# Layer 1's attention product of a four-layer graph network: one product with 128 stationary columns, or two with 64

## The chip, the core and the metric

The kernel runs on one core of a Trainium2 chip. The metric is the device time of one execution, in microseconds (us). The kernel before takes 2623.5 us, the median of three runs (2618.03 to 2626.04). A core has a matrix engine (TensorE, PE in the profile, with its weight loads as PEld), three engines for elementwise work (VectorE or DVE, ScalarE or ACT, GpSimd or POOL), queues that start DMA transfers, an on-chip memory with 128 partitions, and a smaller one, PSUM, into which TensorE writes. A product on TensorE has a stationary operand, loaded first, and a moving operand, streamed through it. The number of columns of the stationary is the number of partitions of the result; the columns of the moving operand are the result's columns.

## What is computed

Sixteen graphs of 1024 nodes go through four layers, x of 1024 x 256 values a graph, with a 0/1 adjacency matrix of 1024 x 1024. Each layer takes `h = relu(layernorm(x))` and adds its result to x. The change is in layer 1:

```python
Wh = jnp.einsum('bnd,de->bne', h, W)
f_i = Wh @ a1
f_j = Wh @ a2
e = jax.nn.leaky_relu(f_i[:, :, None] + f_j[:, None, :], negative_slope=0.2)
e = jnp.where(adj > 0, e, NEG_INF)
alpha = jax.nn.softmax(e, axis=-1)
out = jnp.einsum('bij,bjd->bid', alpha, Wh)
x = x + jax.nn.elu(out)
```

Layer 0 is the same with the softmax over the other axis. Layer 2 averages a linear map of the neighbours and adds a second map. Layer 3 is attention with four heads of 64 columns and a layer norm of its own.

## The kernel before

Everything is in float32. Nodes are cut into NT = 8 blocks of 128, one node of each block to a partition. A graph's layer 1 (`layer1`, line 798) has three phases. First, eight projections (`project`, L686) give `hs`, the rows of Wh with two more columns for f_i and f_j; ScalarE scales them out of PSUM (L802). Then f_j of all nodes is turned into one row, sent through DRAM and broadcast to all partitions (L699 to L711). Then come the weights and the products. For each block j of neighbours VectorE makes `p`, 128 x 1024, one instruction (L822): the exponentials of the masked logits, with neighbours j in the partitions and all 1024 nodes i along the row. ScalarE scales block j of `hs` by a factor of its node (L820); column D of `hs` holds that factor itself, so that the product's last column is the softmax's sum.

The product of output block i sums over j: stationary the 128 columns of `p` that belong to block i, moving the 257 columns of `hs[:, j]`, accumulated in one PSUM bank over the eight j (`product`, line 814, L815). The first two output blocks (EARLY = 2) are multiplied as soon as each `p` is there, so that these products stand among the making of the p's; the other six follow, eight products each. PSUM has two banks for these results (`at_ps`). Each result is read by VectorE (reciprocal of the sum, L836) and by ScalarE twice (L838, L840), and goes to `residual` (line 727). That adds it to x on VectorE (L736, L737), and after every second block starts the next layer's norm: sums of squares on ScalarE (L640), shift and ReLU into `hn` (L667), and TensorE transposes of `hn` (`flip`, L680), whose result ScalarE copies out (L681).

Layer 3's product (line 942) already has the form that the change gives to layer 1. For each p (L929) and each block i, a loop `for c in range(2)` multiplies the 64 columns of `part` of the stationary, with 65 moving columns, into partitions 0 to 63 or 64 to 127 of the result. Layer 0's product (line 759), the projections (L686) and layer 2's products (L877, L883) have stationaries of 128 columns.

All sixteen graphs are generators. Each yields an estimate of the time of the piece just written; a queue ordered by due time (line 1051) resumes the one that is due, and graphs start 120 units apart (`APART`). So layer 1 of one graph is written among layer 3 of the graph before, and its later part beside that graph's tail (line 954) and the first pieces of the graph after it. The framework's planner then orders each engine's instructions by that program order and by what it takes to be ready, and places the waits; instructions wrapped in `later` stay in program order. On each engine the resulting order is fixed. `layer1` yields 1.35 after each block of p and 3.74 after each output block. The mask steps (L575), ScalarE's conversion of the adjacency matrix as it arrives by DMA on the SP queue, belong to the next graph and stand among this on ScalarE's queue.

Of the kernel before, what the change touches and what calls it, by code (L numbers as in the profile page):

```python
# [14 lines left out]
P = 128  # L15
# [406 lines left out]
def tile_simple_stack(  # L422
# [11 lines left out]
    nc = tc.nc  # L434
    B, N, D = x.shape
    NT = N // P
# [246 lines left out]
    def project(norm, w, n, width):  # L683
        ps = mm_ps.tile([P, HALF], F32, tag="mm", name="ps_proj")
        for c in range(DC):
            nc.tensor.matmul(ps[:, :width], norm.ht[:, c, n * P : (n + 1) * P], w[:, c, :width], start=(c == 0), stop=(c == DC - 1))  # L686
        return ps

    def new_hs(name="hs"):
        return state.tile([P, NT, W3], F32, tag="hs", name=name, bufs=3)  # L690

    def spread(col, n, scales, name):

        k = n * NT
        ps = tr_ps.tile([P, P], F32, tag="tr", name="ps_col")
        nc.tensor.transpose(ps[:k, :], col, ident)  # L699
        all_rows = []  # L700
        for scale in scales:
            e = small.tile([H * NT, P], F32, tag="e_row", name="e_row", bufs=2)
            nc.scalar.activation(e[:k, :], ps[:k, :], AF.Exp, scale=scale)
            d = dram.tile([n, N], F32, tag=f"row_{name}", name="d_row", bufs=4)
            later(nc.sync.dma_start(d.rearrange("r (t p) -> (r t) p", p=P), e[:k, :]))
            all_rows += [d[r] for r in range(n)]
        return all_rows

    def everywhere(d, tag):
        row = work.tile([P, N], F32, tag=tag, name="row", bufs=2)  # L710
        later(nc.sync.dma_start(row, d.partition_broadcast(P)))  # L711
        return row

    def column(src, n):

        col = small.tile([P, H, NT], F32, tag="col", name="col", bufs=2)
        nc.vector.tensor_copy(col[:, :n, :], src.rearrange("p t n -> p n t"))
        return col[:, :n, :].rearrange("p n t -> p (n t)")

    def watch(b, layer, terms):  # L720
        k = b * 3 + layer
        nc.vector.tensor_reduce(top[:, k : k + 1], terms, axis=AX.XY, op=OP.max, apply_absolute_value=True)

    def weights(name):
        return work.tile([P, N], F32, tag="p", name=name, bufs=NT)

    def residual(xs, i, v, after, e=None):

        x = xs[:, i, :]
        if i % 2 == 0:  # L730
            if i == NT - 2:
                after.settle()
            after.flip()
            after.sums = small.tile([P, 2], F32, tag="sums", name="sums")
        if e is not None:
            nc.vector.scalar_tensor_tensor(x, e, 1.0, x, op0=OP.min, op1=OP.add)  # L736
        nc.vector.scalar_tensor_tensor(x, v, 0.0, x, op0=OP.max, op1=OP.add, accum_out=after.sums[:, i % 2 : i % 2 + 1])  # L737
        if i % 2:
            after.pair(xs, i // 2, after.sums)
# [58 lines left out]
    def layer1(b, xs, mask, norm, after):  # L798
        hs = new_hs()
        for n in range(NT):  # L800
            ps = project(norm, wx[1], n, D + 2)
            nc.scalar.activation(hs[:, n, : D + 2], ps[:, : D + 2], AF.Copy, scale=norm.rs[n])  # L802
            yield 1.05
        (d_row,) = spread(column(hs[:, :, D + 1 : D + 2], 1), 1, (S - 1.0,), "l1")
        row = everywhere(d_row, "row")
        watch(b, 1, hs[:, :, D : D + 2])
        q = small.tile([P, NT], F32, tag="q", name="q")
        nc.scalar.activation(q, hs[:, :, D], AF.Exp, scale=1.0 - S)
        nc.scalar.activation(hs[:, :, D], hs[:, :, D], AF.Exp, scale=S)
        yield 8.0  # L810
        ps_ = []
        early = [at_ps.tile([P, HALF], F32, tag="at", name="ps_o1") for _ in range(EARLY)]

        def product(ps, i, j):
            nc.tensor.matmul(  # L815
                ps[:, : D + 1], ps_[j][:, i * P : (i + 1) * P], hs[:, j, : D + 1], start=(j == 0), stop=(j == NT - 1)
            )

        for j in range(NT):
            nc.scalar.activation(hs[:, j, :D], hs[:, j, :D], AF.Copy, scale=hs[:, j, D : D + 1])  # L820
            p = weights("p1")
            nc.vector.scalar_tensor_tensor(p, row, q[:, j : j + 1], mask[:, j, :], op0=OP.max, op1=OP.mult)  # L822
            ps_.append(p)
            for i, ps in enumerate(early):
                product(ps, i, j)
            yield 1.35
        for i in range(NT):
            if i < EARLY:
                ps = early[i]
            else:  # L830
                ps = at_ps.tile([P, HALF], F32, tag="at", name="ps_o1")
                for j in range(NT):
                    product(ps, i, j)
            k = b * NT + i
            z = shares[:, k : k + 1]
            nc.vector.reciprocal(z, ps[:, D : D + 1])  # L836
            e = work.tile([P, D], F32, tag="e", name="e")
            nc.scalar.activation(e, ps[:, :D], AF.Exp, scale=z)  # L838
            v = work.tile([P, D], F32, tag="v", name="v")
            nc.scalar.activation(v, ps[:, :D], AF.Copy, scale=z)  # L840
            residual(xs, i, v, after, e)
            yield 3.74
# [232 lines left out]
    ps = tr_ps.tile([P, P], F32, tag="tr", name="ps_bad")  # L1075
# [64 lines left out]
```

## Time and profile before

| | us |
|---|---|
| median of three runs | 2623.5 |
| lowest, highest | 2618.03, 2626.04 |
| span of the profiled execution | 2619.6 |
| TensorE matmul busy (share) | 2456.4 (94%) |
| TensorE weight load busy | 2094.9 (80%) |
| VectorE busy | 1965.3 (75%) |
| ScalarE busy | 1439.9 (55%) |
| layer 3's products, L942, busy | 541.6 |
| layer 1's products, L815, busy | 494.3 |
| layer 0's products, L759, busy | 494.0 |

The span runs from the first to the last instruction of one profiled execution; its time lies between the lowest and the highest of the runs. A float32 product is two instructions in the trace. A row of a group gives the line, the engine, the operation, the operands, the stationary's partitions x columns, the moving operand's partitions x columns, the count, then busy us, the mean ns of one, and the engine's idle time before it with what ended it. The length of one matmul includes its way through the array, and the next starts before it ends, so the time that one costs in a row of them is the distance of two starts. A line of a timeline gives start and length in us of a run of like instructions.

### The profile page before, as it was taken

The numbers are of one execution on the slowest core, as the hardware profiler recorded it, in microseconds if no ns is written. First come the engines' busy times: TensorE is split into PE (matmuls) and PEld (weight loads), VectorE is DVE, ScalarE is ACT, GpSimd is POOL, SyncE is SP. The second block draws the span as 40 slices with busy tenths as digits, with TensorE's granted clock in tenths as the row PEclk, the third lists the DMA queues.
The fourth block names the chain that finished last, engine by engine and source line by source line (L and its number), as shares of the span: only waits on it lengthen the run. The fifth ranks groups of instructions, "written<-read, shape, count | busy, mean of one in ns | idle before, by whom it ended". The sixth has DMA issues, their size and how long they took to land.

```text
span 2619.6 us, 63024 instructions
## 1 busy us (share of the span) xinstructions
PE 2456.4 (94%) x26194; PEld 2094.9 (80%) x26194; DVE 1965.3 (75%) x3815; ACT 1439.9 (55%) x4065; POOL 449.5 (17%) x454
## 2 busy tenths in 40 slices
PE   5799999999999999999999999999999999999975
PEld 4688888888878888787888878888888888878864
DVE  4457778687687977778687787877778687787858
ACT  4564755637565473755637565473755637565350
POOL 1010211203112030211203112030211203011021
PEclk8899999999999999999999999999999999999997
DMA  4541442616225251331615225251432615224021
GB/s 144 126 85 54 107 85 62 133 59 144 53 76 126 70 133 55 108 83 62 134 58 144 57 76 122 70 133 54 124 67 64 137 59 140 66 71 101 26 65 36
DMA packets 212632, 233.76 MB, mean 89 GB/s; under 512 B 10416, under 2 KB 161072, under 8 KB 212336
## 3 DMA queue, kind: packets, MB, share of 16 engines
q1 hardware_dynamic: 74608, 145.73, 17.5%
q0 software_dynamic: 137728, 83.90, 17.5%
q8 instruction: 208, 3.41, 0.5%
q14 instruction: 88, 0.72, 0.1%
HBM read 212.35 MB, written 17.24 MB: 88 GB/s over the span
## 4 chain that ended last, share of the span: by engine, by line
PE 56%; DVE 16%; DMA 12%; ACT 11%; issue 3%; POOL 2%; SPq 0%; DVEq 0%; POOLq 0%; ACTq 0%
PE ps_o L759 15%; PE ps_proj L686 12%; PE ps_o L942 9%; DVE p L929 6%; PE ps_o L883 6%; PE ps_o L815 6%; DMA row<-d_row 5%; PE pt_h L680 5%; DMA raw<-in_adj_t 4%; DVE p L822 4%; ACT mask L575 3%; PE ps_o L877 3%; ACT hn L667 2%; DMA d_row<-e_row 2%; ACT unread L640 2%
## 5 line engine op out<-in xcount | busy, mean ns | idle before, releaser
L929 DVE SCALAR_TENSOR_TENSOR p<-row,q,mask 128x1024 f32<-128x1024 f32 x512 | 631.9, 1278 | 65.4 <-PE ps_o L942 55.7
L942 PEld LDWEIGHTS ps_o<-hb,p 128*64 128x64 f32 x16384 | 505.5, 138 | 102.0 <-DVE p L929 41.2
L942 PE MATMUL ps_o<-hb,p 128*64 128x65 f32 x16384 | 541.6, 224 | 28.9 <-DVE p L929 20.8
L759 PE MATMUL ps_o<-hs,p 128*128 128x256 f32 x2048 | 494.0, 386 | 26.4 <-ACT hs L773 26.0
L686 PE MATMUL ps_proj<-wx,ht 128*128 128x258 f32 (+2 forms) x2048 | 507.8, 388 | 4.0 <-ACT hs L746 2.3
L815 PE MATMUL ps_o<-hs,p 128*128 128x257 f32 x2048 | 494.3, 388 | 14.5 <-ACT mask L575 7.7
L759 PEld LDWEIGHTS ps_o<-hs,p 128*128 128x128 f32 x2048 | 379.7, 191 | 82.8 <-ACT hs L773 30.3
L815 PEld LDWEIGHTS ps_o<-hs,p 128*128 128x128 f32 x2048 | 373.9, 190 | 69.9 <-ACT mask L575 8.3
L686 PEld LDWEIGHTS ps_proj<-wx,ht 128*128 128x128 f32 x2048 | 365.8, 190 | 79.6 <-ACT hs L746 10.4
L592 POOL TENSOR_SCALAR rs<-mv 128x4 f32<-128x4 f32 (+1 forms) x112 | 40.6, 362 | 1555.3 <-ACT unread L640 1542.1
L593 POOL TENSOR_TENSOR rs<-rs,neg_half 128x4 f32<-128x4 f32 (+2 forms) x144 | 261.6, 1818 | 11.7
L736 DVE SCALAR_TENSOR_TENSOR xs<-e,xs 128x256 f32<-128x256 f32 x256 | 108.0, 422 | 182.2 <-ACT e L791 134.1
L667 ACT ACTIVATE hn<-xs,shift 128x256 f32<-128x256 f32 x384 | 175.3, 502 | 123.6 <-DVE shift L635 123.6
L680 PE MATMUL pt_h<-ident,hn 128*128 128x128 f32 x1024 | 180.9, 287 | 43.4 <-ACT hn L667 42.4
L575 ACT ACTIVATE mask<-raw 128x512 uint8<-128x512 int32 x256 | 160.1, 627 | 86.7 <-DMA raw<-in_adj_t 59.5
L883 PE MATMUL ps_o<-hi,adj 128*128 128x258 f32 x1024 | 202.9, 321 | 1.6
L680 PEld LDWEIGHTS pt_h<-ident,hn 128*128 128x128 f32 x1024 | 115.1, 142 | 111.1 <-ACT hn L667 95.0
L585 POOL DMA_DIRECT2D adj<-in_adj x128 | 114.6, 896 | 480.3 <-PE ps_o L883 478.6
L737 DVE SCALAR_TENSOR_TENSOR xs<-v,xs 128x256 f32<-128x256 f32 x384 | 161.0, 422 | 29.5 <-ACT v L793 16.2
L769 DVE SCALAR_TENSOR_TENSOR p<-row,q 128x1024 f32<-128x1024 f32 x128 | 161.4, 1270 | 25.1 <-DMA row<-d_row 25.1
L950 ACT ACTIVATE res<-ps_o 128x260 f32<-128x260 f32 x128 | 46.5, 375 | 228.0 <-PE ps_o L942 227.7
L822 DVE SCALAR_TENSOR_TENSOR p<-row,q,mask 128x1024 f32<-128x1024 f32 x128 | 156.9, 1279 | 10.3 <-DMA row<-d_row 10.1
(108 smaller groups left out, 3000.1 us busy)
## 6 DMA issues: line engine op xcount, KB each, us to landing
raw<-in_adj_t SPq DMA_DIRECT2D x256, 256.0 KB
adj<-in_adj POOLq DMA_DIRECT2D x128, 512.0 KB, 4.9
row<-d_row SPq DMA_DIRECT2D x112, 512.0 KB
xs<-in_x POOLq DMA_DIRECT2D x32, 512.0 KB, 7.1
out<-xs SPq DMA_DIRECT2D x32, 512.0 KB
wx<-in_w SPq DMA_DIRECT2D x3, 256.0 KB
d_row<-e_row SPq DMA_DIRECT2D x48, 4.0 KB
wts<-in_w_t SPq DMA_DIRECT2D x2, 256.0 KB
```

What stands on the lines that cost most here:

```text
L575: nc.scalar.activation(self.bytes[:, n, g * HALF : (g + 1) * HALF], raw, AF.Square, accum_out=squares[:, k : k + 1])
L593: nc.gpsimd.tensor_tensor(rs[:, :n], rs[:, :n], neg_half[:, :n], op=OP.pow)
L667: nc.scalar.activation(hn, xs[:, 2 * g + k, :], AF.Relu, scale=scale, bias=bias)
L680: nc.tensor.transpose(pt[:, c, k * P : (k + 1) * P], hn[:, c * P : (c + 1) * P], ident)
L686: nc.tensor.matmul(ps[:, :width], norm.ht[:, c, n * P : (n + 1) * P], w[:, c, :width], start=(c == 0), stop=(c == DC - 1))
L759: m = nc.tensor.matmul(ps[:, :D], ps_[j][:, i * P : (i + 1) * P], hs[:, j, :D], start=(j == 0), stop=(j == NT - 1))
L769: nc.vector.scalar_tensor_tensor(p, row_a, q[:, j : j + 1], row_b, op0=OP.mult, op1=OP.max)
L815: nc.tensor.matmul(ps[:, : D + 1], ps_[j][:, i * P : (i + 1) * P], hs[:, j, : D + 1], start=(j == 0), stop=(j == NT - 1))
L822: nc.vector.scalar_tensor_tensor(p, row, q[:, j : j + 1], mask[:, j, :], op0=OP.max, op1=OP.mult)
L883: nc.tensor.matmul(ps[:, : D + 2], adj_n[j][:, i, :], h[:, i, : D + 2], start=False, stop=(h is lo and i == NT - 1), skip_group_check=True,)
L929: nc.vector.scalar_tensor_tensor(p, row, q[:, jj, h : h + 1], mask[:, jj, :], op0=OP.max, op1=OP.mult)
L942: nc.tensor.matmul(pss[g][part, k * HW : (k + 1) * HW], ps_[t][:, i * P : (i + 1) * P][:, part], hbv[:, j + t, h, :], start=(j == 0 and t ...
```

## The change

`product` in `layer1` becomes a loop over two halves. Half c takes columns 64c to 64c + 63 of the stationary block and writes partitions 64c to 64c + 63 of the same PSUM bank, with the same moving operand. The results and all that reads them are as before; there are 2048 products in place of 1024, which is 4096 matmul instructions in place of 2048.

```diff
         def product(ps, i, j):
-            nc.tensor.matmul(
-                ps[:, : D + 1], ps_[j][:, i * P : (i + 1) * P], hs[:, j, : D + 1], start=(j == 0), stop=(j == NT - 1)
-            )
+            for c in range(2):
+                part = slice(c * P // 2, (c + 1) * P // 2)
+                nc.tensor.matmul(
+                    ps[part, : D + 1], ps_[j][:, i * P : (i + 1) * P][:, part], hs[:, j, : D + 1],
+                    start=(j == 0), stop=(j == NT - 1),
+                )
```

## The prediction

> **What bounds the kernel now.** I read the page's busy times first, then the groups of instructions by shape, a table of stages, and TensorE's timeline. The page:
>
> ```profile
> PE 2456.4 (94%) x26194; PEld 2094.9 (80%) x26194; DVE 1965.3 (75%) x3815; ACT 1439.9 (55%) x4065; POOL 449.5 (17%) x454
> ```
>
> TensorE is busy 94% of the span, so what the change does to TensorE's time counts, unless it falls in a stretch where another engine is the limit. The groups by shape, for layer 1's product (L815) and layer 3's (L942):
>
> ```profile
> L942 PE MATMUL ps_o<-hb,p 128*64 128x65 f32 x16384 | 541.6, 224 | 28.9 <-DVE p L929 20.8 <-ACT res L950 4.3 <-issue 2.7
> L815 PE MATMUL ps_o<-hs,p 128*128 128x257 f32 x2048 | 494.3, 388 | 14.5 <-ACT mask L575 7.7 <-DVE p L822 5.9 <-ACT v L840 0.7
> ```
>
> The code issues 16 x 8 x 8 = 1024 products in layer 1 and the trace has 2048 matmuls, so each float32 product is two instructions. Layer 1's part in a graph (157 us apart) falls into three stages; the table gives for graph 5 the window, its length, and busy us of PE, PEld, DVE, ACT and POOL:
>
> ```profile
> 879.00:903.00 24.00, 22.67 (x425) 18.91 (x421) 23.96 (x39) 4.81 (x15) 0.00 (x0) 1.00 0.13 47
> 903.00:917.00 14.00, 12.77 (x62) 10.93 (x63) 12.86 (x26) 12.35 (x36) 0.87 (x2) 1.00 0.45 142
> 917.00:928.00 11.00, 11.00 (x59) 9.03 (x58) 7.49 (x22) 10.17 (x25) 8.69 (x7) 1.00 0.00 0
> ```
>
> In the first, layer 1 of one graph runs among layer 3 of the graph before, and DVE is busy 23.96 of 24.00 us: VectorE sets the pace. In the last, TensorE is busy all of 11.00 us. TensorE's timeline over the last two (start, length, instruction, idle before):
>
> ```profile
> 902.91 8.93 PE L815 MATMUL ps_o<-hs,p 128*128 128x257 f32 x40
> 911.68 0.82 PE L680 MATMUL pt_h<-ident,hn 128*128 128x128 f32 x6
> 912.34 3.20 PE L815 MATMUL ps_o<-hs,p 128*128 128x257 f32 x14
> 916.77 0.44 PE L680 MATMUL pt_h<-ident,hn 128*128 128x128 f32 x2 [1.24 <-ACT hn L667]
> 917.05 0.60 PE L815 MATMUL ps_o<-hs,p 128*128 128x257 f32 x2
> 917.48 0.60 PE L680 MATMUL pt_h<-ident,hn 128*128 128x128 f32 x4
> 917.92 3.63 PE L815 MATMUL ps_o<-hs,p 128*128 128x257 f32 x16
> 921.49 0.44 PE L680 MATMUL pt_h<-ident,hn 128*128 128x128 f32 x2
> ...
> 922.64 1.90 PE L815 MATMUL ps_o<-hs,p 128*128 128x257 f32 x8
> 924.38 0.38 PE L680 MATMUL pt_h<-ident,hn 128*128 128x128 f32 x2
> ```
>
> Layer 1's products are cut into runs by transposes (L680) and projections (L686), all with 128 columns of stationary. The one wait, 1.24 us at 916.77, is for ScalarE, which the chain of waits takes through mask steps held by their DMA:
>
> ```profile
> 909.67 3.09 DMA raw<-in_adj_t
> ...
> 916.33 0.40 ACT hn L667
> ```
>
> **What the Trainium skill says.** TensorEngine Tiling (Array Packing), section Key Properties: tiles load and multiply independently, and changing the tiling mode, not just the tile, drains TensorE. The trace agrees with both. Independence: layer 3's halves start 7 ns apart (881.452 and 881.459 in the trace) and the next two 58 ns after; TensorE: Matmul & The Clock Gate, section The mechanism, has about 4 ns. The drain shows where layer 3's narrow form meets a wide one:
>
> ```profile
> 1005.27 2.09 PE L942 MATMUL ps_o<-hb,p 128*64 128x65 f32 x64
> 1007.29 3.29 PE L759 MATMUL ps_o<-hs,p 128*128 128x256 f32 x14
> 1010.51 3.95 PE L942 MATMUL ps_o<-hb,p 128*64 128x65 f32 x128
> 1014.39 0.66 PE L680 MATMUL pt_h<-ident,hn 128*128 128x128 f32 x4
> 1014.89 1.91 PE L686 MATMUL ps_proj<-wx,ht 128*128 128x258 f32 x8
> ```
>
> The same page, section LDWEIGHTS, says that a load costs by its columns, so half as much for 64. The trace agrees: a wide load that nothing hides costs 104 ns (880.388 to 880.709 between two L815 starts, 321 against 217), a narrow one 50 ns (881.452 to 881.560, 108 against 58).
>
> **The change, step by step.**
>
> *Stream.* L815's run of 40 lasts 8.93 us from first start to last end; less 0.38 for the last and 0.10 for its exposed load, 8.45 / 39 = 216.7 ns an instruction. Layer 3's x128 run lasts 3.95 us and its x64 run 2.09, so 64 instructions more cost 1.86 us: 58.1 ns per pair of halves, that is, the halves do run side by side. From transposes 128 wide (917.48 to 917.92, four in 0.44 us: 109 ns) to 257 wide (216.7) a column costs 107.7 / 129 = 0.835 ns. A pair of halves at 257 columns is then 58.1 + 192 x 0.835 = 218.4 ns, where one whole instruction takes 216.7. The 2048 instructions become 2048 such pairs: +1.7 ns each, 3.5 us; 40 of a graph's 128 lie under VectorE in the first stage, which leaves 2.4. Unhidden weight loads of 64 instead of 128 columns are in the switches below; all others lie under the stream (138 ns against 218).
>
> *Switches.* From the five lines above: the x64 run takes 1007.29 - 1005.27 = 2.02 us (2.01 in its neighbours) where its stream is 1.86: 0.15, of which 0.05 is its first load and 0.10 the drain on leaving. The wide run of 14 takes 3.22 where 14 x 0.216 = 3.02: 0.20, of which 0.10 is its first load and 0.09 the drain. L680's run of four takes 0.50 after a narrow run, 0.44 elsewhere: 0.06 for its load. So entering the narrow form costs 0.143 (0.093 + 0.05), leaving it costs 0.203 into a wide product and 0.155 into a transpose. Counting L815's neighbours in the whole timeline: L942 to L815 120 times, L815 to L942 105; into L815 from L680, L686 or L699 95 times, out of it to L680 or L686 110. With L815 narrow, the first two kinds vanish: 120 x 0.203 + 105 x 0.143 = 39.4 us of TensorE. The last two become switches: 95 x 0.143 + 110 x 0.155 = 30.6 us.
>
> *Where they fall.* The vanishing ones lie in the first stage, under VectorE. They are worth nothing there, except the last: at 902.91 TensorE takes over as the limit, and one exit of 0.2 is saved, 15 x 0.2 = -3. If TensorE were the limit there, they would be worth the whole 39.4. Of the new ones, three a graph (out at 911.68, in at 912.34, out at 916.77: 0.45 us) lie before the wait for hn, which hides them: 15 x 0.45 = 6.8 off, leaving 23.8. The hiding costs 6.8 if ScalarE comes earlier. The rest, five entries and five exits after 917 (0.72 + 0.78 = 1.5 us), lie where TensorE is 11.00 of 11.00 us busy. The chain goes on from there through L686, the next row's broadcast and L759, so that delay moves everything after.
>
> *Lone halves.* The two halves are separate instructions to whatever orders the program. If a transpose falls between them, one streams alone for 0.434 us, and each run with an odd number of halves costs 0.217 more. The trace of before can't show it for L815. Bounds: none (0) to all seven runs of all 16 graphs (24 us). Of layer 3's fourteen runs in a graph, two are odd (x10 and x18: five and nine halves of two instructions); at that share, 7 x 16 x 0.143 x 0.217 = 3.5. I take 3.5.
>
> *The rest.* No wait, DMA, tile or operation on another engine is added or moved. L836, L838 and L840 wait for the second half's last instruction, which ends with the first's. 2048 more matmuls and loads are fetched; layer 3 shows four times that issued every 58 ns a pair, so I price it at nothing.
>
> Sum: 2.4 + 23.8 - 3 + 3.5 = +26.7 us, on a span of 2619.6: 2646.3. The runs' median is 2623.5, 3.9 above that span, so 2650.2; I say 2650.
>
> **Rivals.**
> 1. *The vanished switches pay* (not slower). Place: the first stage. In its last rounds TensorE needs 3.08 us (starts 899.83 and 902.91) and VectorE about as much, so if TensorE is what sets the pace, up to 39.4 comes off: 2623.5 + 2.4 + 23.8 + 3.5 - 39.4 = 2614; at half of that, 2634. It brings the old time back once three quarters (29.7 of 39.4) are realized, and the 0.3% band from 21.8. For it: the near tie. Against it: DVE 23.96 of 24.00, and TensorE waits there for VectorE.
> 2. *Lone halves and another order.* The order on the queues shifts with twice the products, most runs are odd and transposes sit deeper: +24 instead of 3.5, and as much again from runs cut once more (3 round trips of 0.3 us a graph, 14 us): about 2685. Layer 3's odd runs speak for it, its x64 runs against.
> 3. *The halves don't overlap at 257 columns*: the second stream costs 2048 x 0.217 = 444 us, of which little is covered: about 3065. Layer 3's 58 ns a pair speaks against it; its streams fill 54 of those 58 ns (65 x 0.835), so the operand's reads already run at full rate.
>
> **How the numbers follow.** Chances: the forecast 0.60 (its own range 2634 to 2668), rival 1 0.22 (2608 to 2634), rival 2 0.14 (2668 to 2710), rival 3 0.04. A measurement of this kernel can't tell less than about 0.3%, 7.9 us, from no change. Faster, below 2615.6, is the end of rival 1 where all of it pays and more of the new switches hide before a wait: 0.07. Same, to 2631.4, is most of its rest plus a little of the forecast's edge: 0.17. Slower: 0.76. The range of 8 in 10 leaves out rival 3, the upper half of rival 2 and the bottom of rival 1: 2613 to 2690.
>
> **What would show it.** After: L815 as 128*64, x4096, in pairs about 218 ns apart; no extra 0.2 us between L942 and L815, and about 0.3 us a round trip between L815 and L680. The first stage stays near 24 us with more idle TensorE; the last grows by about 1.5 us. I am wrong if the first stage shortens by more than 1 us, if the pairs pace at over 230 ns, or if L815's runs have odd counts of halves throughout.

## The result, and the profile after

The changed kernel takes 2667.2 us (2665.3 to 2669.7, four runs), the kernel before in the same series 2624.3: a ratio of 1.0164 (95% interval 1.015 to 1.0177), 43 us slower. The forecast was 2650, 27 slower. The way was right, the size too small.

The groups of instructions by shape, after (lines moved: L817 is layer 1's product, L945 layer 3's, L825 and L932 their p's):

```profile
L945 PE MATMUL ps_o<-hb,p 128*64 128x65 f32 x16384 | 540.4, 224 | 47.2 <-DVE p L932 35.4 <-issue 5.6 <-ACT res L953 4.3
L817 PE MATMUL ps_o<-hs,p 128*64 128x257 f32 x4096 | 515.3, 386 | 14.7 <-DVE p L825 14.0 <-ACT v L843 0.7
```

Twice the instructions are busy 515 us instead of 494. The halves do overlap. Layer 3 waits 35.4 us for its p instead of 20.8: TensorE has more time to spare beside VectorE. The stages of graph 5, after (window, its length, busy us of PE, PEld, DVE, ACT and POOL, then the granted clock, the DMA share and GB/s):

```profile
895.00:919.00 24.00, 21.39 (x480) 17.69 (x478) 23.97 (x37) 4.07 (x12) 0.00 (x0) 1.00 0.14 50
919.00:933.00 14.00, 13.08 (x126) 8.43 (x123) 13.57 (x29) 12.29 (x35) 0.00 (x0) 1.00 0.48 152
933.00:948.00 15.00, 14.24 (x103) 8.39 (x100) 7.77 (x24) 11.71 (x31) 9.19 (x8) 1.00 0.00 0
```

In a window of the same 24 us over the first stage VectorE is busy for 23.97, as before, and TensorE for less (21.39 instead of 22.67). What follows has grown from 25 us to 29. The windows are set by eye; the table below measures the stages. TensorE's timeline over it, after:

```profile
917.41 2.09 PE L945 MATMUL ps_o<-hb,p 128*64 128x65 f32 x64 [0.19 <-DVE p L932]
919.32 9.27 PE L817 MATMUL ps_o<-hs,p 128*64 128x257 f32 x82
928.53 0.87 PE L680 MATMUL pt_h<-ident,hn 128*128 128x128 f32 x6
929.33 0.65 PE L817 MATMUL ps_o<-hs,p 128*64 128x257 f32 x2
930.90 0.44 PE L680 MATMUL pt_h<-ident,hn 128*128 128x128 f32 x2 [0.92 <-ACT hn L667]
931.26 3.68 PE L817 MATMUL ps_o<-hs,p 128*64 128x257 f32 x30
934.87 0.66 PE L680 MATMUL pt_h<-ident,hn 128*128 128x128 f32 x4
935.46 3.69 PE L817 MATMUL ps_o<-hs,p 128*64 128x257 f32 x32
939.43 0.44 PE L680 MATMUL pt_h<-ident,hn 128*128 128x128 f32 x2 [0.28 <-ACT hn L667]
...
942.23 0.44 PE L680 MATMUL pt_h<-ident,hn 128*128 128x128 f32 x2 [0.48 <-ACT hn L667]
```

Four things can be read here. A half product is two instructions, so x82 is 41 halves, x2 one and x30 fifteen: odd numbers, with a half that streams alone at the end. Runs of layer 1 and of transposes now change the tiling at each border: the four transposes at 934.87 take 0.59 us to the next start, the four of before at 917.48 took 0.44. From 917.41, layer 3's x64 run passes into layer 1 after 1.91 us (0.05 of it for the first load, after a wait), where with a change to a wide product it took 2.01: no drain. And the one wait for `hn` has become three.

From the starts of TensorE's instructions in the two traces I summed the same stretches for graphs 1 to 14 (means, us a graph):

| | before | after |
|---|---|---|
| layer 1's first product to what follows layer 3's last | 22.44 | 21.92 |
| from there to what follows layer 1's last product | 24.27 | 27.85 |
| ... the streams of its instructions | 22.34 | 22.78 |
| ... halves that stream alone | 0 | 1.08 |
| ... drains and bare loads at changes of tiling | 0.10 | 2.15 |
| ... waits and the rest | 1.83 | 1.84 |
| distance of two graphs | 156.92 | 159.92 |

The second stretch grows by 3.58 us: 2.05 for changes of tiling, 1.08 for lone halves, 0.44 for work that moved into it, while the first gets 0.52 shorter. The distance of two graphs grows by 3.0 us. Over fifteen distances that is 45 us, where the runs differ by 43 and the two profiled executions (2619.6 and 2667.9) by 48.

### The profile page after: what moved, and what is told of

It reads as the page before. It is cut to its first block, busy times and chain, and to the rows that moved or that the text cites. A ratio compares the mean times of both kernels' runs of the same rounds, so it can differ in the third digit from the quotient of the medians.

```text
span 2667.9 us, 67173 instructions
## 1 busy us (share of the span) xinstructions
PE 2487.0 (93%) x28242; PEld 2017.5 (76%) x28242; DVE 1968.1 (74%) x3815; ACT 1443.4 (54%) x4065; POOL 431.7 (16%) x454
## 4 chain that ended last, share of the span: by engine, by line
PE 53%; DVE 17%; ACT 13%; DMA 9%; issue 4%; POOL 3%; SPq 0%; DVEq 0%; POOLq 0%; ACTq 0%
PE ps_o L759 15%; PE ps_proj L686 12%; PE ps_o L945 9%; PE ps_o L886 8%; DVE p L932 7%; DVE p L825 5%; DMA raw<-in_adj_t 4%; PE pt_h L680 4%; ACT hn L667 3%; PE ps_o L817 3%; DMA row<-d_row 3%; PE ps_o L880 3%; ACT unread L640 2%; ACT mask L575 2%; POOL rs L593 2%
## 5 line engine op out<-in xcount | busy, mean ns | idle before, releaser
L932 DVE SCALAR_TENSOR_TENSOR p<-row,q,mask 128x1024 f32<-128x1024 f32 x512 | 632.4, 1280 | 65.2 <-PE ps_o L945 55.7
L945 PEld LDWEIGHTS ps_o<-hb,p 128*64 128x64 f32 x16384 | 509.1, 138 | 117.4 <-DVE p L932 61.0
L945 PE MATMUL ps_o<-hb,p 128*64 128x65 f32 x16384 | 540.4, 224 | 47.2 <-DVE p L932 35.4
L817 PE MATMUL ps_o<-hs,p 128*64 128x257 f32 x4096 | 515.3, 386 | 14.7 <-DVE p L825 14.0
L759 PE MATMUL ps_o<-hs,p 128*128 128x256 f32 x2048 | 498.3, 387 | 16.1 <-ACT hs L773 15.5
L759 PEld LDWEIGHTS ps_o<-hs,p 128*128 128x128 f32 x2048 | 377.1, 192 | 73.0 <-ACT hs L773 21.7
L817 PEld LDWEIGHTS ps_o<-hs,p 128*64 128x64 f32 x4096 | 300.8, 138 | 153.6 <-issue 30.2
L592 POOL TENSOR_SCALAR rs<-mv 128x4 f32<-128x4 f32 (+1 forms) x112 | 35.4, 316 | 1610.2 <-ACT unread L640 1595.6
L593 POOL TENSOR_TENSOR rs<-rs,neg_half 128x4 f32<-128x4 f32 (+2 forms) x144 | 248.4, 1732 | 9.5
L886 PE MATMUL ps_o<-hi,adj 128*128 128x258 f32 x1024 | 210.5, 324 | 2.9 <-ACT hi L872 2.8
L886 PEld LDWEIGHTS ps_o<-hi,adj 128*128 128x128 f32 x1024 | 153.1, 190 | 22.2 <-ACT hi L872 11.3
```

What stands on the lines that cost most here:

```text
L593: nc.gpsimd.tensor_tensor(rs[:, :n], rs[:, :n], neg_half[:, :n], op=OP.pow)
L759: m = nc.tensor.matmul(ps[:, :D], ps_[j][:, i * P : (i + 1) * P], hs[:, j, :D], start=(j == 0), stop=(j == NT - 1))
L817: nc.tensor.matmul(ps[part, : D + 1], ps_[j][:, i * P : (i + 1) * P][:, part], hs[:, j, : D + 1], start=(j == 0), stop=(j == NT - 1),)
L886: nc.tensor.matmul(ps[:, : D + 2], adj_n[j][:, i, :], h[:, i, : D + 2], start=False, stop=(h is lo and i == NT - 1), skip_group_check=True,)
L932: nc.vector.scalar_tensor_tensor(p, row, q[:, jj, h : h + 1], mask[:, jj, :], op0=OP.max, op1=OP.mult)
L945: nc.tensor.matmul(pss[g][part, k * HW : (k + 1) * HW], ps_[t][:, i * P : (i + 1) * P][:, part], hbv[:, j + t, h, :], start=(j == 0 and t ...
```

## The experiments

The theory: a change of tiling costs 0.14 to 0.20 us, but only where TensorE is the limit; two halves stream in the time of one whole product; a half without its partner streams alone. Rival A: changes of tiling cost wherever they fall. Rival B: halves are slower by their number. Rival C: the loss is a new order of work with new waits. Times below are ratios to the kernel before, run beside each one.

**e1_early: only the two early blocks in halves.** It changes what stands in VectorE's stage and nothing else.

```diff
         def product(ps, i, j):
+            if i >= EARLY:
+                nc.tensor.matmul(ps[:, : D + 1], ..., hs[:, j, : D + 1], start=(j == 0), stop=(j == NT - 1))
+                return
             for c in range(2):
```

> Only the two early output blocks (i below EARLY) are multiplied in halves; the other six stay wide. By the planner's order 75 entries and 75 exits between layer 3's narrow products and layer 1's vanish (26 us of TensorE at 0.203 and 0.143), all in the stage where VectorE is busy throughout, and no new switch arises. My theory (switches cost only where TensorE is the limit; a pair of halves streams in a whole one's time): 0 to 5 us faster than before, 2619 to 2624. Rival A (switches cost wherever they fall): 26 us faster, about 2598. Rival B (halves are slower in themselves, by their number): slower than before by a quarter of the change's 43 us, about 2635.

Measured: 2625.9 us, ratio 1.0012 (1.0004 to 1.002). 150 changes of tiling fewer, and no gain: it is 1 to 5 us slower, where I had set 0 to 5 us faster. Its first stage, which begins about 7.75 us later in its trace than in that of before, shows why there is nothing to gain (same columns as above):

```profile
886.75:910.75 24.00, 21.50 (x440) 18.60 (x441) 23.92 (x42) 5.60 (x17) 0.00 (x0) 1.00 0.12 42
```

TensorE's busy time falls from 22.67 to 21.50, and VectorE is at 23.92 of 24.00 as before. Over the whole span layer 3's products wait 32.2 us for their p, where they waited 20.8: what TensorE saves there it spends waiting. Rivals A and B both fall.

**e2_late: only the six late blocks in halves.**

```diff
+            if i < EARLY:
+                nc.tensor.matmul(ps[:, : D + 1], ..., hs[:, j, : D + 1], start=(j == 0), stop=(j == NT - 1))
+                return
```

> The other way round: the two early blocks stay wide, the six late ones are multiplied in halves. The late blocks' new switches and the halves cut apart by transposes are all there; 75 entries and 75 exits in VectorE's stage come back. My theory: as slow as the changed kernel or up to 5 us slower, 2666 to 2672. Rival A (switches cost wherever they fall): 26 us slower than the changed kernel, about 2693. Rival B (by the number of halves): three quarters of the change's 43 us, about 2656.

Measured: 2668.0 us, ratio 1.017 (1.0153 to 1.0188). The whole loss of the change, without its early part; bringing back 150 changes of tiling in VectorE's stage added nothing. With e1 this places the loss.

**e3_pairs: the second half pinned behind the first.**

```diff
             for c in range(2):
                 part = slice(c * P // 2, (c + 1) * P // 2)
-                nc.tensor.matmul(
+                with tc.high_priority() if c else ExitStack():
+                    half = nc.tensor.matmul(
...
+                    if c:
+                        later(half)
```

> The change, with the second half of each product pinned right behind the first (a higher priority and an edge to the instruction before it). The planner's order then has no narrow run with an odd number of halves, where the change has 62; the number of switches is the same, 428. My theory (a lone half streams for 0.434 us where its half share of a pair is 0.217): 62 x 0.217 = 13.5 us faster than the changed kernel, about 2653. Rival C (the loss beyond the switches is a new order of work in which TensorE waits for ScalarE's hn, lone halves being free): the same as the changed kernel, 2663 to 2670.

Measured: 2656.9 us, ratio 1.0133 (1.0115 to 1.015): 10 us faster than the change (2667.2; 8 by the two ratios), between the 13.5 of the theory and the nothing of rival C. TensorE's timeline shows even numbers of halves at every change of tiling, and what took part of the gain:

```profile
914.42 8.84 PE L818 MATMUL ps_o<-hs,p 128*64 128x257 f32 x80
923.19 0.88 PE L680 MATMUL pt_h<-ident,hn 128*128 128x128 f32 x6
923.99 0.65 PE L818 MATMUL ps_o<-hs,p 128*64 128x257 f32 x4
926.07 0.44 PE L680 MATMUL pt_h<-ident,hn 128*128 128x128 f32 x2 [1.42 <-ACT hn L667]
```

The 41 halves of the change took from 919.32 to 928.53, 9.21 us; 40 take 8.77. But the wait for `hn` is 1.42 us instead of 0.92. Summed as in the table, the lone halves fall from 1.08 us a graph to 0 and waits and the rest rise from 1.84 to 2.57. So lone halves cost 1.08 a graph in TensorE's time, 16 us over fifteen graphs, and some 10 us in all; the remainder of their room went into waits for ScalarE.

**e5_single: six of eight second halves left out.** Rows 64 to 127 of each result sum over two blocks of neighbours instead of eight, so three eighths of layer 1's multiplications are gone.

```diff
-            for c in range(2):
+            for c in range(2 if j < 2 else 1):
...
-                    start=(j == 0), stop=(j == NT - 1),
+                    start=(j == 0), stop=(j == (1 if c else NT - 1)),
```

> The second half of each product is left out for six of the eight blocks j, so that rows 64 to 127 of every result sum over two blocks only; the first halves are as in the change. If a half alone takes as long as a whole product, and the second halves are free beside it, TensorE's stream is that of the change without lone halves: with the switches of the changed kernel (432 by the planner's order) 2645 to 2658. If the second halves cost time of their own, layer 1's products shrink by three eighths and the time falls below the kernel before, under 2600.

Measured: 2643.3 us, ratio 1.0083 (1.0068 to 1.0099). That is 2 us below the theory's band and far above the other. By layer 1's busy time three eighths would be 185 us. They buy 24 against the change, and 14 against e3. In its trace first halves alone start 217 ns apart, as whole products do: the second half is all but free when its partner is there, and half a product alone is no cheaper than a whole one.

**e8_apart: eight first halves, then eight second halves.**

```diff
                 ps = at_ps.tile([P, HALF], F32, tag="at", name="ps_o1")
-                for j in range(NT):
-                    product(ps, i, j)
+                for c in range(2):
+                    for j in range(NT):
+                        product(ps, i, j, (c,))
```

> The change, with each late block's sixteen half products in another order: eight for the first half, then eight for the second, so that neighbours in TensorE's order lie in the same tile. If halves run side by side only when they are neighbours in the order (my theory), each takes its own 0.434 us: 16 x 6 x 8 x 0.434 = 333 us more in the stage that TensorE bounds, with the lone halves' 10 us no longer counted apart: about 2990. If TensorE takes halves from further down its queue, or if the second half is simply free, it stays near 2667.

Measured: 2849.6 us, ratio 1.0871 (1.0851 to 1.0891). Far slower, but by 182 us against the change and not by 323. The long run in its timeline:

```profile
976.18 15.18 PE L817 MATMUL ps_o<-hs,p 128*64 128x257 f32 x88
```

88 instructions in pairs would take 9.5 us, one by one 19.1. In the trace each tile's turn of sixteen lasts 2.65 us, not 16 x 0.217 = 3.47: at its end two series of starts run side by side (977.048 and 977.054, then 977.264 and 977.321, and so on for four of each). The trace doesn't name the tile, but in the planner's order eight products of one half stand before eight of the other throughout this run, so when a tile has some three instructions left in the queue, the other tile's first ones already start. So neighbours overlap, and nearly neighbours too, over about three instructions: 6 x 16 blocks x 2 x 2.65 us is 177 us more than the same in pairs. My "only when neighbours" was too strict.

**e7_flips: transposes in halves as well.** On top of e3, for the two norms that are transposed among layer 1's products.

```diff
-                    nc.tensor.transpose(pt[:, c, k * P : (k + 1) * P], hn[:, c * P : (c + 1) * P], ident)
+                    if self.narrow:
+                        halves(pt[:, c, k * P : (k + 1) * P], hn[:, c * P : (c + 1) * P], ident, start=True, stop=True)
```

> The run with pinned halves, with narrow transposes too (pinned halves against the same identity) for the two norms that are transposed among layer 1's products. By the planner's order the switches between layer 1 and transposes, 199 in the run with pinned halves, are gone; in all there are 280 instead of 428, none of them between layers 1 and 3. The streams are the same, with as many pairs. My theory (a switch where TensorE is the limit costs 0.14 to 0.20 us): 148 x 0.147 = 22 us faster than the run with pinned halves (2656.9), about 2635. Rival C (the rest of the loss is the new order of work and its waits): no change from 2656.9, or slower by what the 1024 more instructions cost.

Measured: 2691.7 us, ratio 1.0283 (1.0261 to 1.0304): slower than e3 where the theory said faster. The groups by shape show a mistake in the experiment (L464 is the helper that makes both halves, L692 the wide transposes that stayed):

```profile
L464 PE MATMUL pt_h<-ident,hn 128*64 128x128 f32 x2048 | 144.9, 282 | 52.4 <-ACT hn L676 49.9
...
L692 PE MATMUL pt_h<-ident,hn 128*128 128x128 f32 x512 | 88.9, 284 | 5.4 <-ACT hn L676 5.4
```

A wide transpose is one instruction; 512 of them became 2048, since a product with the identity is two instructions a half. In pairs that is 1024 x 0.109 us where there were 512 x 0.109: 56 us more. (The Trainium skill, TensorEngine Tiling (Array Packing), section Feature Incompatibilities, has transpose mode on float32 as excluded with column tiling, which fits; no run here tries it.) 56 less the expected 22 is 34, and the two runs differ by 35, or 39 by their ratios. That sum was made afterwards, so e7 agrees with the price of a switch but doesn't show it. The next two runs do.

**e9_switches_late and e10_switches_covered: switches alone, in the kernel before.** Six products a graph in pinned halves, scattered among wide ones, in blocks 6 and 7 or in blocks 3 and 4.

```diff
+            mm = halves if i in (6, 7) and j in (1, 3, 5) else nc.tensor.matmul
-            nc.tensor.matmul(
+            mm(
```

> The kernel before with three of the eight products (j of 1, 3 and 5) of the output blocks 6 and 7 in pinned halves, the rest wide: 96 entries and 96 exits more than before, no lone half, the streams the same. These blocks come after the wait for ScalarE's hn, where TensorE is busy throughout. My theory: 96 x (0.143 + 0.203) = 33 us slower than before, about 2656. If a switch costs nothing of its own and the change lost its time to a new order and its waits (rival C): within 5 us of before.

> The same six products a graph in halves, but in the output blocks 3 and 4, ahead of that wait: again 96 entries and 96 exits. They are 2.1 us a graph of TensorE; the wait of 1.2 us behind them takes up what it can. My theory: 33 less 16 x 1.2 = 19, so about 14 us slower than before, 2637; the limits are 5 (all covered, the wait being longer in other graphs) and 33 (the wait only moves).

Measured: 2646.6 us, ratio 1.0081 (1.0065 to 1.0096), and 2636.1, ratio 1.0037 (1.0023 to 1.005), beside 2626.6. So 20 and 9.5 us, where I had 33 and 14. TensorE's timeline of e9 has the price by itself:

```profile
452.04 0.65 PE L464 MATMUL ps_o<-hs,p 128*64 128x257 f32 x4
452.63 0.70 PE L824 MATMUL ps_o<-hs,p 128*128 128x257 f32 x2
453.26 0.65 PE L464 MATMUL ps_o<-hs,p 128*64 128x257 f32 x4
```

From 452.04 to 453.26 a product in halves and a wide one take 1.22 us, where their streams are 4 x 0.217 = 0.87: 0.35 a round trip, the 0.346 of the prediction. What fails is the exposure. Summed as in the table, changes of tiling cost 2.0 us a graph more in e9 than before, waits and the rest fall from 1.83 to 1.40, and two graphs stand 1.36 further apart, 20 us over fifteen. So a third of the price is taken up, most of it by waits in this same stretch, even after the wait that I took for the last. In e10 waits and the rest fall to 0.41. TensorE's waits for `hn` over the whole span (us, times, longest), before, in e9 and in e10:

```profile
PE pt_h L680 <- ACT hn L667: 42.4, 38, 3.8
```

```profile
PE pt_h L688 <- ACT hn L675: 37.4, 40, 3.8
```

```profile
PE pt_h L688 <- ACT hn L675: 29.7, 27, 3.8
```

In e9 they fall by 5 us and in e10 by 13: cover, as the theory has it. In the change they rise (while layer 0's waits for ScalarE fall, from 26.0 us to 15.5):

```profile
PE pt_h L680 <- ACT hn L667: 48.7, 68, 2.6
```

**b3_layer3_entry and b2_without_flips: the same price, saved.** The prediction's count says where switches would be worth removing: where layer 3 begins, among wide products, with TensorE at its limit. Layer 1's attention products stay wide; its projections and layer 0's last output block go into pinned halves. b3 also puts the last transposes before layer 1 in halves; b2 leaves them.

```diff
+            mm = halves if w is wx.get(1) else nc.tensor.matmul
+            mm(ps[:, :width], norm.ht[:, c, n * P : (n + 1) * P], w[:, c, :width], ...)
...
+            if i == NT - 1:
+                halves(ps[:, :D], ps_[j][:, i * P : (i + 1) * P], hs[:, j, :D], ...)
+                return
```

> The kernel before, layer 1's attention products wide as there, with halves (pinned) for what stands among layer 3's products where TensorE is the limit: layer 1's projections, the last output block of layer 0, and the last transposes before layer 1. By the planner's order the switches outside VectorE's stage fall from 197 to 49; the 225 between layers 1 and 3 stay. My theory: 148 x 0.147 = 22 us faster than before, about 2602. Rival A' (the stage in which layer 3 begins is bound by VectorE too): no change from before. Rival B (halves are slower in themselves): slower than before by some 10 us.

> The run on layer 3's entry (8 us faster than before) with its transposes wide again, since in it a transpose in halves was two products of two instructions each, where a wide transpose is one instruction. Switches outside VectorE's stage: 81 by the planner's order, where before has 197 and that run had 49. My theory: 116 x 0.147 = 17 us faster than before, about 2605. If that stage has covers of its own, as the half size of the earlier gain suggests: 8 to 10 us, 2612.

Measured: b3 2613.8 us, ratio 0.9968 (0.9954 to 0.9982); b2 2610.6, ratio 0.9938 (0.9926 to 0.995), 16 us faster than the kernel before beside it, where the theory had 17. It beats both kernels. Its timeline, to set beside the prediction's lines of that stage:

```profile
1014.70 2.03 PE L956 MATMUL ps_o<-hb,p 128*64 128x65 f32 x64
1016.57 2.79 PE L464 MATMUL ps_proj<-wx,ht 128*64 128x258 f32 x24
1019.18 2.03 PE L956 MATMUL ps_o<-hb,p 128*64 128x65 f32 x64
```

The x64 run passes on after 1.87 us, where it was 2.01 to 2.02, and starts without its bare load. That b3 gained only half is partly its transposes in halves (64 more pairs, 7 us, against 5 for 32 switches); the other 5 or 6 us between b3 and b2 are not explained by a run here.

## Why the prediction was right, and where it was short

*Stream: right.* Two halves of 257 columns start 7 ns apart and every 216.7 ns in the trace after, as a whole product does. The forecast's 1.7 ns more a pair isn't there, so its 2.4 us are nothing. Rival 3, no overlap, is out; e5 shows the overlap from the other side.

*Vanished switches worth nothing: right.* e1 and e2 show it from both sides, and rival 1 is out. The saving of one exit a graph, -3, can't be told apart in the first stage's 22.44 to 21.92, part of which is work that moved.

*Price of a switch: right.* 0.35 us a round trip in e9 against 0.346; b2, with 116 switches fewer, gains 16 us where that price gives 17.

*Number of switches: short.* Counted as in the prediction, the trace after has 108 entries and 123 exits of layer 1 at wide work, not 95 and 110. The planner, given twice as many pieces, cut layer 1's products into eight runs a graph instead of seven: the last one now stands behind the last transpose, ahead of the projections. At the prediction's prices that is 3.9 us.

*Cover of 6.8 us before the wait for `hn`: failed.* It exists in the kernel before: e10 shows it at work. But the change doesn't keep that kernel's order. The planner placed the transposes anew, TensorE waits for `hn` at three places in graph 5 instead of one, and waits and the rest are 1.84 us a graph after 1.83. So nothing of what the switches cost was taken up; that the new order is the reason is argued, not shown by a run.

*Lone halves: right in kind, a third of the size.* The 3.5 us were taken from layer 3's share of odd runs. e3 gives 10; by the trace it was 1.08 us a graph, five of eight runs odd in graph 5. Layer 3's runs were a poor sample, probably because a p feeds 32 instructions there (16384 for 512 p's) and most runs are whole groups of them, while a transpose comes in wherever the planner takes its `hn` to be ready.

With these terms, 26.7 - 2.4 + 3.9 + 6.8 + 6.5 makes 41.5, against 43. With the trace's 16 us for lone halves in place of e3's 10 it makes 48, which is what the two profiled executions differ by. The measured time lies less than 1 us inside the upper end of the forecast's own range, next to rival 2, which had lone halves as its start; of rival C's new waits the change itself shows no net gain or loss. Of the signs of being wrong, the first stage got 0.5 us shorter and not more than 1, the pairs start 217 ns apart and not over 230, and odd runs are common but not throughout.

Left open: why the waits stay at 1.8 us a graph in the change and rise to 2.6 in e3, while in e9 they take up part of the price. A run with the planner's order of before and halves in place of wholes would tell, and wasn't made.

## What to carry to other kernels

A change of form has to be priced at its borders: count what stands next to each run on the engine, on both sides and stage by stage, since the same switch is free where another engine sets the pace (e1, e2) and costs up to its full price where this one does (20 of 33 us in e9, 16 of 17 in b2). Splitting an instruction also gives whatever orders the program new places to cut; what must stay together has to be pinned together. And a wait found in the old order is no safe cover for a change that brings another order: here the waits were as long afterwards.

## What the runs showed that I had not expected

TensorE starts the other tile's products about three instructions before the queue reaches them (2.65 us for sixteen half-product instructions of 0.217 in e8). A float32 transpose is one instruction at 109 ns and a product with the identity two, so a transpose in halves costs twice the stream (56 us in e7, by count). Three eighths of a layer's multiplications were worth 14 us in e5, against e3.
